# A graph kernel of four layers, last layer: the order in which its last five row blocks are prepared, summed and finished

## The chip, the cores and the metric

The kernel runs on one core of a Trainium2 chip. A core has five engines that run side by side, each through its own queue of instructions in order: TensorE (PE in the profile, with PEld for its weight loads), VectorE (DVE), ScalarE (ACT), GpSimd (POOL) and SyncE (SP), which here only starts DMA transfers. An instruction waits for semaphores that other engines or transfers raise, and what stands behind it on the same engine waits with it. The metric is the device time of one launch in microseconds; lower is better.

## The reference

Four layers work on a feature matrix `x` of 2708 rows and 512 columns with one sparse adjacency matrix `adj` of 2708 by 2708. Each layer is a sum over neighbours, a nonlinearity, and a residual with layer normalisation. Only the last layer matters here:

```python
bw = sign(weight)                     # 512 x 512
ba = maximum(sign(x), 0)
xw = ba @ bw.T                        # whole numbers
x  = layernorm(x + relu(adj @ xw))    # mean and variance of a row, eps 1e-5
```

## The kernel before

The rows are cut into 22 blocks of 128 (block 21 has 20). The adjacency matrix is never multiplied whole. For a block `b`, the columns that hold anything were listed in the first layer, and the matching rows of `adj` were packed into `packed[b]`, tiles of 128 listed columns by the block's rows. `ROOM[b]` is the number of such tiles, `DIRECT` names column tiles that are taken whole. In the last layer `xw_rows` in memory holds `xw` in 16 bit.

**Sums.** A block's sum `l3_b` is built on PE in one bank of PSUM (pool `ps_3`, three of them). It consists of:

- its own diagonal: `dp` (two matrices, a high and a low part of the diagonal, made by ACT at L2122 and by DVE at L2125) times its own rows `xo`, fetched by SP at L2114 and widened to 32 bit by `widened`, which uses DVE every third time (L2036) and ACT otherwise (L2038). The products are at L2130;
- its tiles: four at a time, `halves_of` splits `packed[b]` into a high half (ACT, L2025) and a low half (DVE, L2026), and each tile is multiplied twice (L2141) with the rows that POOL gathered (`gather3`, L626) or with rows that lie in SBUF.

The five densest blocks, 0 to 4, are not gathered. Their five sums (`whole`, five banks) grow together, one column tile at a time, in `whole_tile(j)`: 22 steps of ten products (L2102), spread between the other blocks by a count of tiles (`due`). The last of the 22 falls after block 15, so blocks 16 to 20 run with nothing between them.

**Finishing.** `finish3(b, ps, more)` adds the relu of the sum to the old features (L2049), takes the statistics of a row (L2051, L2053), and notes them in `moments`. With `more` it stops there, so that the next block joins it. Otherwise it takes the root for the one or two blocks noted: the constant is added (L2060), ACT takes a square root (L663), DVE improves its reciprocal in a few tiny steps (`newton`, L680 to L683) and forms the offset (L2062). ACT then scales each block (L2066) and SP writes it out (L2070). In the tail before the change the pairs are 15 and 16, 17 and 0, 18 and 1, 19 and 2, then 20 alone, then 3 and 4.

**Order.** The code above is traced in program order, and a scheduler then arranges the instructions of each engine by estimated times; it moves work of a later block ahead of an earlier one and the reverse. `in_order()` is a context in which each engine keeps the traced order: every instruction gets an ordering edge to the one traced before it on its engine. Before the change it is used in the first layer, not here. SP's transfers take part in this as well: a DMA issue is an instruction of SP's queue.

**Buffers** that the tail uses: `xo` 2, `dp` 2, widened rows 4, split halves (`parts`) 4, gathered tiles 11, sums 3, `rs3` 2, `mv3` 3.

Of the kernel before, what the change touches and what calls it, by code (L numbers as in the profile page):

```python
# [8 lines left out]
F32 = mybir.dt.float32  # L9
# [4 lines left out]
AF = mybir.ActivationFunctionType  # L14
ALU = mybir.AluOpType
# [4 lines left out]
P = 128  # L20
# [39 lines left out]
WHOLE3 = 5  # L60
# [447 lines left out]
def sparse_layers(ctx, tc, x, adj, adj_t, w0_t, b0, w_sa, a_sa, w_gcnb, b_gcnb, wa, ba, wb, bb, w3_t,  # L508
# [11 lines left out]
    nc = tc.nc  # L520
    N, D = x.shape
    KC = D // P
    NB = -(-N // P)
# [4 lines left out]
    def rows(b: int) -> int:  # L528
        return min(P, N - b * P)

    def direct(b: int):

        return tuple(range(NB)) if b == 0 else DIRECT.get(b, ())

    def tiles(b: int) -> int:
        return len(direct(b)) + ROOM[b]
# [3 lines left out]
    small = ctx.enter_context(tc.tile_pool(name="s_small", bufs=4))  # L540
    dram = ctx.enter_context(tc.tile_pool(name="s_dram", bufs=1, space=DRAM))

    f = [feat.tile([P, D], F32, tag=f"f{b}", name=f"f{b}") for b in range(NB)]
# [115 lines left out]
    def rsqrt_of(dst, v, m: int, n: int, name: str):  # L659

        r = small.tile([P, 2, 4], F32, tag="rsqs", name=f"rsqs_{name}")
        r0, r1 = r[:m, 0, :n], r[:m, 1, :n]
        nc.scalar.activation(r0, v, AF.Sqrt)  # L663
        newton(dst, v, r0, r1, n)

    def newton(dst, v, r0, r1, n: int):

        for step_ in newton_steps(dst, v, r0, r1, n):
            step_()
# [49 lines left out]
    with tc.tile_pool(name="s_pre", bufs=1) as pre:  # L719
# [33 lines left out]
        for d in (y_rows, x1_rows, x2_rows, xw_rows):  # L753
# [16 lines left out]
            out=tri, in_=tri, pattern=[[1, P]], compare_op=ALU.is_gt, fill=0.0, base=0,  # L770
# [5 lines left out]
            out=step, in_=ident, pattern=[[1, P]], compare_op=ALU.not_equal, fill=-1.0,  # L776
# [8 lines left out]
        turn_at, at = {}, 0  # L785
# [35 lines left out]
        b = 0  # L821
        while b < NB:
# [6 lines left out]
            b = end  # L829
# [1184 lines left out]
    with tc.tile_pool(name="s_l3", bufs=11, reuse_waits="tile") as lp, \  # L2014
            tc.tile_pool(name="s_ps_w", bufs=1, reuse_waits="tile", space=PSUM) as ps_w, \
            tc.tile_pool(name="s_ps_3", bufs=3, reuse_waits="tile", space=PSUM) as ps_3:
        W3 = WHOLE3 * P
        CH3 = 4
        PW = max(CH3 * P, W3)

        def halves_of(a, r: int, w: int, name: str):

            p = lp.tile([P, 2, PW], F32R, tag="parts", name=f"p{name}", bufs=4)
            low, high = p[:r, 0, :w], p[:r, 1, :w]
            nc.scalar.copy(high, a)  # L2025
            nc.vector.tensor_tensor(low, a, high.bitcast(F32), op=ALU.subtract)  # L2026
            return p

        turn = [0]

        def widened(t, r: int, name: str, tag: str = "wide", bufs: int = 4):

            g = lp.tile([P, D], F32R, tag=tag, name=f"w{name}", bufs=bufs)
            turn[0] += 1
            if turn[0] % 3 == 0:
                nc.vector.tensor_copy(g[:r], t[:r])  # L2036
            else:
                nc.scalar.copy(g[:r], t[:r])  # L2038
            return g

        moments = []

        def finish3(b: int, ps, more: bool):

            m = rows(b)
            old = place_of_x(b)
            k = len(moments)
            t = old[:, :D]
            nc.vector.scalar_tensor_tensor(t[:m], ps[:m], 0.0, t[:m], op0=ALU.max, op1=ALU.add)  # L2049
            st = small.tile([P, 6], F32, tag="st", name=f"st_3_{b}")  # L2050
            nc.vector.bn_stats(st[:m], t[:m])  # L2051
            mv = moments[0][2] if k else lp.tile([P, 2, 2], F32, tag="mv3", name=f"mv_3_{b}", bufs=3)
            nc.vector.bn_aggr(mv[:m, k, :], st[:m])  # L2053
            moments.append((b, t, mv))
            if more:
                return
            n = len(moments)
            rs = lp.tile([P, 2, 2], F32, tag="rs3", name=f"rs_3_{b}", bufs=2)
            mean, v = mv[:m, :n, 0], mv[:m, :n, 1]
            nc.vector.tensor_scalar(v, v, LN_EPS, None, op0=ALU.add)  # L2060
            rsqrt_of(rs[:m, 0, :n], v, m, n, f"3_{b}")
            nc.vector.scalar_tensor_tensor(  # L2062
                rs[:m, 1, :n], mean, -1.0, rs[:m, 0, :n], op0=ALU.mult, op1=ALU.mult
            )
            for k, (b, t, _) in enumerate(moments):
                nc.scalar.activation(  # L2066
                    t[:m], t[:m], AF.Identity, bias=rs[:m, 1, k : k + 1],
                    scale=rs[:m, 0, k : k + 1],
                )
                nc.sync.dma_start(out[b * P : b * P + m, :], t[:m])  # L2070
            moments.clear()

        sources3 = {}

        def gather3(b: int):
            sources3[b] = [gathered(lp, D, xw_rows, b, t, F32R) for t in range(ROOM[b])]

        order3 = [NB - 1, *range(WHOLE3, NB - 1)]
        gather3(order3[0])
        gather3(order3[1])  # L2080


        whole = [ps_w.tile([P, D], F32, tag=f"w{b}", name=f"l3_{b}") for b in range(WHOLE3)]

        xw_direct = {0: xw0}

        def whole_tile(j: int):
            r = rows(j)
            if j:
                g = lp.tile([P, D], F16, tag="xs", name=f"xs{j}", bufs=4)  # L2090
                nc.sync.dma_start(g[:r], xw_rows[j * P : j * P + r, :])
                g = widened(g, r, f"s{j}", "wide" if j > 1 else "wide1", 4 if j > 1 else 1)
                if j == 1:
                    xw_direct[1] = g
            else:
                g = xw0
            a = lp.tile([P, W3], F32, tag="aw", name=f"aw{j}", bufs=4)
            nc.sync.dma_start(a[:r], adj_t[j * P : j * P + r, :W3])
            p = halves_of(a[:r], r, W3, f"w{j}")
            for b in range(WHOLE3):  # L2100
                for h in range(2):
                    nc.tensor.matmul(  # L2102
                        whole[b], p[:r, h, b * P : (b + 1) * P], g[:r, :],
                        start=(j == 0 and h == 0), stop=(j == NB - 1 and h == 1),
                    )
        j = 0
        while j < AHEAD3:
            whole_tile(j)
            j += 1
        due = 0  # L2110
        for at, b in enumerate(order3):
            m = rows(b)
            xo = lp.tile([P, D], F16, tag="xo", name=f"xo{b}", bufs=2)
            nc.sync.dma_start(xo[:m], xw_rows[b * P : b * P + m, :])  # L2114
            xo = widened(xo, m, f"o{b}")
            if at + 1 < len(order3) and at:
                gather3(order3[at + 1])
            src = [xw_direct[j] for j in direct(b)] + sources3.pop(b)
            ps = ps_3.tile([P, D], F32, tag="mm", name=f"l3_{b}")

            dp = lp.tile([P, 2, P], F32R, tag="dp", name=f"dp{b}", bufs=2)
            nc.scalar.activation(  # L2122
                dp[:m, 1, :m], ident[:m, :m], AF.Copy, scale=dia_own[:m, b : b + 1]
            )
            nc.vector.scalar_tensor_tensor(  # L2125
                dp[:m, 0, :m], ident[:m, :m], dia_own[:m, b : b + 1],
                dp[:m, 1, :m].bitcast(F32), op0=ALU.mult, op1=ALU.subtract,
            )
            for h in range(2):
                nc.tensor.matmul(  # L2130
                    ps[:m], dp[:m, h, :m], xo[:m, :], start=(h == 0), stop=False
                )
            for i0 in range(0, tiles(b), CH3):
                n = min(CH3, tiles(b) - i0)
                p = halves_of(
                    packed[b][:, i0 : i0 + n, :].rearrange("p n i -> p (n i)"), P, n * m,
                    f"{b}_{i0}",
                )
                for i in range(n):
                    for h in range(2):  # L2140
                        nc.tensor.matmul(  # L2141
                            ps[:m], p[:, h, i * m : (i + 1) * m], src[i0 + i],
                            start=False, stop=(i0 + i == len(src) - 1 and h == 1),
                        )
            pending = bool(moments)
            finish3(b, ps, not pending and b not in (order3[0], order3[-1]))
            if j == NB and whole and len(moments) == 1:
                finish3(WHOLE3 - len(whole), whole.pop(0), False)
            due += ROOM[b]
            while j < NB and due >= FETCHES3:  # L2150
                whole_tile(j)
                j += 1
                due -= FETCHES3
        while whole:
            finish3(WHOLE3 - len(whole), whole.pop(0), len(whole) % 2 == 1)


@with_exitstack
# [74 lines left out]
```

## Time and profile before

| what | value |
|---|---|
| median of 9 runs | 957.8 us (954.47 to 960.23) |
| the profiled execution's own time | 955.83 us |
| its span | 954.0 us |
| mean granted TensorE clock | 0.961 |
| busy: PE, DVE, POOL, ACT | 852.7, 648.0, 548.1, 382.8 us |
| last layer's sums, first product to last | about 837.5 to 942.2 us |
| last block of the whole tiles ends | 924.4 us |
| last output issued | 948.5 us |

The span is the time from the first to the last event of the core; the execution's own time has 1.83 us more around it. Times in the profile count from the span's start. In lists of groups or of a timeline a line reads: start and length in us, engine, line of the program, operation, the tile written, an arrow, the tiles read, sizes, and the number of instructions merged into the line. In brackets stands how long the engine had been idle before it and what released it. `SPq` marks the issue of a transfer on SP's queue. Timeline lines of one kind that follow each other on their engine are merged, so a length can include short gaps. Matmul ends are modelled.

### The profile page before, as it was taken

How to read it: one execution, taken by the hardware profiler on the slowest of the kernel's cores; microseconds unless marked ns; L12 is line 12 of the kernel's file. 1: busy time of each engine (PE TensorE's matmuls, PEld its weight loads, DVE VectorE, ACT ScalarE, POOL GpSimd, SP SyncE). 2: the span in 40 equal slices, each digit the busy share in tenths (PEclk: the TensorE clock that was granted, in tenths of full speed). 3: DMA queues.
4: the chain of work that ended last, by engine and by line, in shares of the span. 5: the costliest groups of instructions: out<-in, count | busy, mean ns of one | idle time of the engine just before them, and what ended most of it. 6: DMA issues, size and time to landing. Idle time of an engine off the chain costs nothing.

```text
span 954.0 us, 12778 instructions
## 1 busy us (share of the span) xinstructions
PE 852.7 (89%) x3659; PEld 449.4 (47%) x3659; DVE 648.0 (68%) x2440; ACT 382.8 (40%) x812; POOL 548.1 (57%) x660
## 2 busy tenths in 40 slices
PE   1897998589999989999999979989999999689993
PEld 1444553122223334565555534544556455368872
DVE  4898887846677846556544447576888776557676
ACT  2675665100000115545444434334444433255664
POOL 2688888788888577777532054543454320067662
PEclk9999899889999979999999999999999999889998
DMA  9999996567777657776643277886787541299985
GB/s 264 363 344 328 351 309 189 165 199 219 229 226 231 207 167 209 219 239 207 191 151 122 101 259 262 277 283 230 238 304 258 171 145 49 83 299 353 342 250 191
DMA packets 93556, 220.05 MB, mean 231 GB/s; under 512 B 13660, under 2 KB 28364, under 8 KB 93476
## 3 DMA queue, kind: packets, MB, share of 16 engines
q0 software_dynamic: 43008, 127.61, 44.5%
q1 hardware_dynamic: 38520, 76.78, 23.5%
q10 hardware_dynamic: 11948, 14.76, 4.9%
q8 instruction: 31, 0.51, 0.2%
q14 instruction: 49, 0.40, 0.1%
HBM read 178.21 MB, written 31.71 MB: 220 GB/s over the span
## 4 chain that ended last, share of the span: by engine, by line
PE 65%; DMA 10%; DVE 9%; POOL 5%; issue 3%; ACT 1%; SPq 0%; ACTq 0%; DVEq 0%; POOLq 0%
PE l L1396 15%; PE h L1622 8%; PE e L1847 6%; PE a L1847 6%; PE l L2102 6%; PE l L2141 4%; PE pg L1895 4%; PE pc L1895 3%; DMA xg<-y_rows,i 3%; DMA arow<-in_adj_dram 2%; PE e L1655 2%; PE a L1656 2%; POOL a L1099 2%; DMA xg<-x_rows,i 2%; PE px L1956 2%
## 5 line engine op out<-in xcount | busy, mean ns | idle before, releaser
L1099 POOL DMA_INDIRECT a<-in_adj_t_dram,row_at x98 | 108.0, 1102 | 49.7 <-issue 21.7
L626 POOL DMA_INDIRECT xg<-x_rows,i x98 | 96.2, 982 | 66.7 <-PE l L1396 39.4
L626 POOL DMA_INDIRECT xg<-y_rows,i x98 | 98.7, 1007 | 25.3 <-issue 18.2
L1396 PE MATMUL l<-xg,a 128*32 128x512 f32 (+3 forms) x196 | 92.6, 624 | 16.7 <-DMA xg<-y_rows,i 16.5
L1823 POOL DMA_INDIRECT xg<-x_rows,i x60 | 59.5, 992 | 61.2 <-ACT ae L1578 16.5
L626 POOL DMA_INDIRECT xg<-xw_rows,i x70 | 70.9, 1012 | 35.4 <-issue 12.0
L1823 POOL DMA_INDIRECT a<-x_rows,i x38 | 37.1, 977 | 88.8 <-DVE mask L1581 37.0
L1133 PE MATMUL y<-s_w,xt 128*128 128x512 f32 (+1 forms) x176 | 87.1, 641 | 0.0
L1622 PE MATMUL h<-s_wsa,xt 128*128 128x256 f32 (+3 forms) x352 | 81.9, 385 | 0.0
L1622 PEld LDWEIGHTS h<-s_wsa,xt 128*128 128x128 f32 (+1 forms) x352 | 63.8, 186 | 24.8 <-ACT xt L1617 12.5
L840 ACT ACTIVATE unused<-arow 128x1408 uint8<-128x1408 f32 (+3 forms) x44 | 58.5, 1329 | 11.9 <-DMA arow<-in_adj_dram 6.7
L1847 PE MATMUL a<-xg,a 128*32 128x512 f32 (+2 forms) x120 | 48.9, 609 | 4.5 <-DMA xg<-x_rows,i 4.5
L663 ACT ACTIVATE rsqs<-mv 128x1 f32<-128x1 f32 (+2 forms) x56 | 11.3, 202 | 101.9 <-DVE mv L692 97.8
L1133 PEld LDWEIGHTS y<-s_w,xt 128*128 128x128 f32 (+1 forms) x176 | 33.8, 203 | 37.5 <-issue 37.2
L1396 PEld LDWEIGHTS l<-xg,a 128*32 128x32 f32 (+3 forms) x196 | 20.6, 143 | 64.9 <-DMA xg<-y_rows,i 44.8
L2102 PE MATMUL l<-ws,pw 128*128 128x512 f32 (+1 forms) x210 | 50.1, 392 | 0.0
L1847 PE MATMUL e<-xg,ae 128*32 128x512 f32 (+2 forms) x120 | 47.9, 601 | 1.3 <-ACT ae L1583 1.3
L694 POOL TENSOR_TENSOR rs<-mv,s_neg_half 128x1 f32<-128x1 f32 (+1 forms) x22 | 13.0, 590 | 60.0 <-DVE mv L692 51.1
L1895 PE MATMUL pg<-s_wg,pt 128*128 128x256 f32 (+1 forms) x176 | 44.8, 395 | 1.3 <-ACT pt L1883 1.3
L688 DVE BATCH_NORM_STATS2 st<-t 128x6 f32<-128x512 f32 (+1 forms) x66 | 45.3, 686 | 0.3
L904 DVE TENSOR_SCALAR s_mask<-arow 128x1300 bf16<-128x1300 f32 (+5 forms) x42 | 38.0, 910 | 9.8 <-DMA arow<-in_adj_dram 9.8
L2102 PEld LDWEIGHTS l<-ws,pw 128*128 128x128 f32 (+1 forms) x210 | 39.7, 190 | 8.8 <-DVE rs L2062 0.4
(310 smaller groups left out, 1958.4 us busy)
## 6 DMA issues: line engine op xcount, KB each, us to landing
arow<-in_adj_dram SPq DMA_DIRECT2D x21, 704.0 KB, 7.4
arow<-in_adj_dram SPq DMA_DIRECT2D x21, 650.0 KB, 6.5
x_rows<-f SPq DMA_DIRECT2D x40, 256.0 KB, 3.7
aw<-in_adj_t_dram SPq DMA_DIRECT2D x21, 320.0 KB, 4.2
y_rows<-yt ACTq DMA_DIRECT2D x20, 256.0 KB, 5.5
x_rows<-h SPq DMA_DIRECT2D x19, 257.0 KB, 2.6
f<-in_x_dram SPq DMA_DIRECT2D x19, 256.0 KB, 7.1
h_own<-x_rows SPq DMA_DIRECT2D x19, 256.0 KB
```

Source lines behind the costliest of these rows:

```text
L626: nc.gpsimd.indirect_dma_start(out=t, out_offset=None, in_=src[:, :], in_offset=bass.IndirectOffsetOnAxis(ap=index[b][:, i : i + 1], axis=0),)
L688: nc.vector.bn_stats(st[:m], t[:m])
L840: nc.scalar.activation(unused[:m, : ar.shape[1]], ar, AF.Copy, accum_out=row_sums[:m, b, h : h + 1])
L1099: nc.gpsimd.indirect_dma_start(out=packed[b][:, t + len(direct(b)), :], out_offset=None, in_=adj_t, in_offset=bass.IndirectOffsetOnAxis(ap ...
L1133: nc.tensor.matmul(ps[:m], xt[:, k, :m], w0[:, k, :], start=(k == 0), stop=(k == KC - 1))
L1396: nc.tensor.matmul(ps[r0:r1], weights, moving, start=(i == order[0]), stop=last_of(b, i, order))
L1622: nc.tensor.matmul(ps, xt[:, k, :m], w[:, k, :], start=(k == 0), stop=(k == KC - 1))
L1823: nc.gpsimd.indirect_dma_start(out=g, out_offset=None, in_=x2_rows[:, :], in_offset=bass.IndirectOffsetOnAxis(ap=index[b][:, t : t + 1], a ...
L1847: nc.tensor.matmul(ps[r0:r1], weights, moving, start=(i == order[0]), stop=last_of(b, i, order))
L1895: nc.tensor.matmul(ps, pt[:, k, :m], w[:, k, :], start=(k == 0), stop=(k == KC - 1))
L2102: nc.tensor.matmul(whole[b], p[:r, h, b * P : (b + 1) * P], g[:r, :], start=(j == 0 and h == 0), stop=(j == NB - 1 and h == 1),)
L2141: nc.tensor.matmul(ps[:m], p[:, h, i * m : (i + 1) * m], src[i0 + i], start=False, stop=(i0 + i == len(src) - 1 and h == 1),)
```

## The change

The body of the loop over the blocks is cut into functions, and the loop is split in two. Up to block 15 (while column tiles of the whole blocks are left) a block is done as before: `ready` (own rows and diagonal), the next block's gathers, `products3` (which splits the tiles four at a time as it goes), `finish3`.

For blocks 16 to 20 everything is traced inside `in_order()`:

- `all_parts(b)` makes all operands of a block: the fetch of its own rows, their widening, its diagonal, both halves of all its tiles. It is called for block 16 before the loop, and for block `b + 1` after the products of `b` and ahead of the finishing of `b`.
- `finish3` takes the square root on ACT, then calls `between`, and only then does the tiny steps, the scaling and the output. In blocks 16 to 19 `between` is the first half of finishing one whole block (sum, statistics), which stays in `moments` for the next turn.
- The pairs are now 15 and 16, 0 and 17, 1 and 18, 2 and 19, then 3 and 4, then 20 alone.

```diff
-        def finish3(b: int, ps, more: bool):
+        def finish3(b: int, ps, more: bool, between=None):
...
             n = len(moments)
+            done = list(moments)
+            moments.clear()
...
-            rsqrt_of(rs[:m, 0, :n], v, m, n, f"3_{b}")
-            nc.vector.scalar_tensor_tensor(
-                rs[:m, 1, :n], mean, -1.0, rs[:m, 0, :n], op0=ALU.mult, op1=ALU.mult
-            )
-            for k, (b, t, _) in enumerate(moments):
...
+            r = small.tile([P, 2, 4], F32, tag="rsqs", name=f"rsqs_3_{b}")
+            r0, r1 = r[:m, 0, :n], r[:m, 1, :n]
+            nc.scalar.activation(r0, v, AF.Sqrt)
+
+            def apply():
+                newton(rs[:m, 0, :n], v, r0, r1, n)
+                nc.vector.scalar_tensor_tensor(
+                    rs[:m, 1, :n], mean, -1.0, rs[:m, 0, :n], op0=ALU.mult, op1=ALU.mult
+                )
+                for k, (b, t, _) in enumerate(done):
+                    nc.scalar.activation(
+                        t[:m], t[:m], AF.Identity, bias=rs[:m, 1, k : k + 1],
+                        scale=rs[:m, 0, k : k + 1],
+                    )
+                    nc.sync.dma_start(out[b * P : b * P + m, :], t[:m])
+
+            if between:
+                between()
+            apply()
...
-        for at, b in enumerate(order3):
+        ready3 = {}
+
+        def ready(b: int):
             m = rows(b)
             xo = lp.tile([P, D], F16, tag="xo", name=f"xo{b}", bufs=2)
             nc.sync.dma_start(xo[:m], xw_rows[b * P : b * P + m, :])
             xo = widened(xo, m, f"o{b}")
...
+            ready3[b] = (xo, dp, [])
+
+        def ready_part(b: int, i0: int):
+            n = min(CH3, tiles(b) - i0)
+            ready3[b][2].append(halves_of(
+                packed[b][:, i0 : i0 + n, :].rearrange("p n i -> p (n i)"), P, n * rows(b),
+                f"{b}_{i0}",
+            ))
...
+        def all_parts(b: int):
+            ready(b)
             for i0 in range(0, tiles(b), CH3):
...
+                ready_part(b, i0)
...
+        at = 0
+        while j < NB:
+            b = order3[at]
+            ready(b)
+            if at:
+                gather3(order3[at + 1])
+            ps = products3(b)
+            finish3(b, ps, not moments and at > 0)
+            at += 1
             due += ROOM[b]
             while j < NB and due >= FETCHES3:
                 whole_tile(j)
                 j += 1
                 due -= FETCHES3
-        while whole:
-            finish3(WHOLE3 - len(whole), whole.pop(0), len(whole) % 2 == 1)
+
+        def finish_whole(more: bool):
+            finish3(WHOLE3 - len(whole), whole.pop(0), more)
+
+        with in_order():
+            all_parts(order3[at])
+            while at < len(order3):
+                b = order3[at]
+                at += 1
+                if at < len(order3):
+                    gather3(order3[at])
+                ps = products3(b)
+                if at < len(order3):
+                    all_parts(order3[at])
+                else:
+                    while whole:
+                        finish_whole(len(whole) > 1 and not moments)
+                left = whole and at < len(order3)
+                finish3(
+                    b, ps, not moments and at < len(order3),
+                    (lambda: finish_whole(True)) if left else None,
+                )
```

More of the change, by code (lines that the diff above doesn't have):

```diff
@@ L2060, in finish3 @@
             nc.vector.tensor_scalar(v, v, LN_EPS, None, op0=ALU.add)
-            rsqrt_of(rs[:m, 0, :n], v, m, n, f"3_{b}")
-            nc.vector.scalar_tensor_tensor(
-                rs[:m, 1, :n], mean, -1.0, rs[:m, 0, :n], op0=ALU.mult, op1=ALU.mult
-            )
-            for k, (b, t, _) in enumerate(moments):
-                nc.scalar.activation(
-                    t[:m], t[:m], AF.Identity, bias=rs[:m, 1, k : k + 1],
-                    scale=rs[:m, 0, k : k + 1],
-                )
-                nc.sync.dma_start(out[b * P : b * P + m, :], t[:m])
-            moments.clear()
+            r = small.tile([P, 2, 4], F32, tag="rsqs", name=f"rsqs_3_{b}")
[5 more added lines that the diff above has]
+                    rs[:m, 1, :n], mean, -1.0, rs[:m, 0, :n], op0=ALU.mult, op1=ALU.mult
+                )
+                for k, (b, t, _) in enumerate(done):
[7 more added lines that the diff above has]
+            apply()
         sources3 = {}
@@ L2115, in sparse_layers @@
             xo = widened(xo, m, f"o{b}")
[L2116 to L2119, printed above, removed]
             dp = lp.tile([P, 2, P], F32R, tag="dp", name=f"dp{b}", bufs=2)
@@ L2128, in sparse_layers, with products3 @@
             )
+            ready3[b] = (xo, dp, [])
[5 more added lines that the diff above has]
+            ))
+        def products3(b: int):
+            m = rows(b)
+            src = [xw_direct[j] for j in direct(b)] + sources3.pop(b)
+            ps = ps_3.tile([P, D], F32, tag="mm", name=f"l3_{b}")
+            xo, dp, parts = ready3.pop(b)
             for h in range(2):
@@ L2132, in sparse_layers @@
                 )
-            for i0 in range(0, tiles(b), CH3):
[L2134 to L2148, printed above, removed]
+            for i in range(tiles(b)):
+                if i // CH3 == len(parts):
+                    ready3[b] = (xo, dp, parts)
+                    ready_part(b, i)
+                    ready3.pop(b)
+                p, k = parts[i // CH3], i % CH3
+                for h in range(2):
+                    nc.tensor.matmul(
+                        ps[:m], p[:, h, k * m : (k + 1) * m], src[i],
+                        start=False, stop=(i == len(src) - 1 and h == 1),
+                    )
+            return ps
+        def all_parts(b: int):
+            ready(b)
+            for i0 in range(0, tiles(b), CH3):
+                ready_part(b, i0)
[8 more added lines that the diff above has]
+            at += 1
             due += ROOM[b]
```

## The prediction

> **What bounds the kernel now.** I read the slices of the page first, then the busy times over two stretches of the end, then the chain of waits, then the timeline of the same stretch engine by engine. The change touches only what is issued for blocks 16 to 20, so the end is what matters.
>
> Two stretches (start:end, length, then busy us and instruction count of PE, weight loads, DVE, ACT, POOL, then PE clock, DMA share, GB/s):
>
> ```profile
> 920.00:940.00 20.00, 16.73 (x65) 12.70 (x63) 17.81 (x63) 9.95 (x22) 10.65 (x11) 0.91 0.80 225
> 940.00:954.00 14.00, 2.13 (x8) 1.42 (x8) 5.92 (x31) 6.50 (x11) 0.00 (x0) 0.69 0.47 174
> ```
>
> PE is all but done at 940. DVE is the fuller engine in the last 20 us: 17.81 of 20. The chain of waits (start, us) says the same:
>
> ```profile
> 929.44 2.30 PE l L2141 x10
> 935.42 1.19 DVE st L2051 x2
> 940.07 2.14 PE l L2141 x8
> 942.96 1.29 DVE st L2051 x2
> ```
>
> So the end is already a DVE chain, with one excursion to PE: the last block's products. The timeline shows why PE stood still before it:
>
> ```profile
> 939.33 0.69 DVE L2026 TENSOR_TENSOR p<-a,p 128x512 fp32r<-128x512 f32 x1
> 940.07 0.73 PE L2141 MATMUL l<-xw,p 128*128 128x512 f32 x2 [3.35 <-DVE p L2026]
> ```
>
> The low half of block 20's operand stood on DVE behind the finishing of 16 to 19, and PE waited 3.35 us for it. That is the visible prize. Next, one pair being finished (13 and 14), which gives the prices of the steps, and the outputs on SP's queue that follow it:
>
> ```profile
> 918.43 0.68 DVE L2051 BATCH_NORM_STATS2 st<-f 128x6 f32<-128x512 f32 x1
> 919.14 0.18 DVE L2053 BATCH_NORM_AGGREGATE mv<-st 128x2 f32<-128x6 f32 x1
> 919.36 0.17 DVE L2060 TENSOR_SCALAR mv<-mv 128x2 f32<-128x2 f32 x1
> ...
> 919.72 0.20 ACT L663 ACTIVATE rsqs<-mv 128x2 f32<-128x2 f32 x1
> ...
> 920.01 0.15 DVE L680 RECIPROCAL rsqs<-rsqs 128x2 f32<-128x2 f32 x1
> ...
> 921.63 0.16 DVE L2062 SCALAR_TENSOR_TENSOR rs<-mv,rs 128x2 f32<-128x2 f32 x1
> 921.83 1.52 ACT L2066 ACTIVATE f<-f,rs 128x512 f32<-128x512 f32 x2
> ```
>
> ```profile
> 913.23 0.33 SPq L2114 DMA_DIRECT2D xo<-xw_rows  x1
> 915.40 0.33 SPq L2114 DMA_DIRECT2D xo<-xw_rows  x1
> 920.11 0.80 SPq L2114 DMA_DIRECT2D xo<-xw_rows  x2
> 922.67 1.04 SPq L2070 DMA_DIRECT2D out_dram<-f  x2
> ```
>
> What to see: the four loads of xo, for blocks 17 to 20, are all issued before the outputs of 13 and 14. No block of the tail waits for its own rows. DMA issues of the end (KB each, median us to landing):
>
> ```profile
> out_dram<-f SPq DMA_DIRECT2D x13, 256.0 KB, 3.0
> xs<-xw_rows SPq DMA_DIRECT2D x20, 128.0 KB, 4.4
> ```
>
> **The change part by part.** Laying the two built orders beside each other: on all five engines nothing moves up to block 15, apart from line numbers, and no instruction is added or dropped. The split of the root (square root, then the rest after the whole block) and the new pairs (15+16, 0+17, 1+18, 2+19, 3+4, 20 alone) keep six roots in the tail, as before. These edits cost nothing by themselves; everything lies in the order of 16 to 20.
>
> *The prize.* Block b+1's operands now stand ahead of block b's finishing, so the 3.35 us of PE disappear.
>
> *SP's queue.* The order is now: xo17, outputs 13, 14, 15, 16, xo18, outputs 0, 17, xo19, outputs 1, 18, xo20, and so on. SP issues in order, and an output waits for its L2066 on ACT. So xo18 is issued only when block 16 is finished, xo19 only after 17, xo20 only after 18. Behind xo18 stands a widening on DVE, at the head of DVE's order, and behind that dp18, p18 and all of block 17's finishing. For xo19 and xo20 the widening is on ACT, ahead of dp and p there, and DVE's dp, p and the next finishing wait for ACT. That is a closed loop: finish b-1, output, load xo of b+1, operands of b+1, finish b. Nothing runs ahead of it.
>
> *One turn of the loop*, from L2049 of block b to L2049 of b+1. L2049 to statistics 0.72 (942.24 to 942.96, block 20), to aggregate 0.71, to the added constant 0.22 (rows above): 1.65. Then the whole block in between: 0.10 to its L2049, 0.72, 0.71, and 0.20 to the reciprocal: 3.38. The root on ACT (0.36 + 0.29) hides under the whole block's 1.7 us. From the reciprocal to L2062 five steps of 0.20 (921.04, 921.23, 921.43, 921.63 are such starts), 1.0; 0.20 to ACT: 4.58. From ACT's first L2066 to the end of the second output's issue 1.88 (921.83 to 923.71), 0.10 to xo's issue: 6.56. Landing: the trace has no landing for xo. Bounds are 2.0 us, the fastest DMA that touches x_rows, and 4.4, the median of xs, the same rows and size at a DMA share over 1. I take 3.0, the outputs' own median here, because the queue is as empty in the loop as in this stretch: 9.56. Then the operands. With DVE widening: 0.46, dp 0.40, p 0.69, so 1.55. With ACT widening: 0.53, dp 0.33, high half 0.62, then DVE's low half 0.75, so 2.25 (starts at 914.23, 914.76, 915.28; lengths of L2025 and L2026). A turn is 11.1 us for 18, and 11.8 for 19 and 20.
>
> *The sum.* Block 16's products end where they did: whole tile 21 still ends at 924.4, the half clock from 924.8 to 928.1 remains, and p16 is ready at 924.0. L2049 of 16 stays at 929.0. Then 17 at 929.0 + 11.1 = 940.1, 18 at 951.9, 19 at 963.7. From there: 4.38 to L2062 of pair 2+19 (968.1). Block 4 follows: 0.1 + 0.72 + 0.71 + 0.22 + 0.36 + 0.29 + 1.0 = 3.4 (971.5). Block 20: 0.1 + 0.72 + 0.71 + 0.22 + 0.36 + 0.29 + 0.8 (one column, four steps) = 3.2 (974.7). Then 0.2 to ACT, 0.8 for L2066, 0.05 to the issue: 975.75. In the trace of before the last output is issued at 948.52 and the span ends at 954.0, 5.48 later: 981.2. That is 27.2 us over 954.0. The profiled execution took 955.83, 1.83 around its span, and the median of the nine is 957.8. I add the difference to the median: 985.0.
>
> *What is covered.* The whole blocks' five L2049, which ran from 922.09 while PE was busy, now stand inside the turns; they are counted there. Gathers (POOL) of 18 to 20 wait for tiles that 15 to 17 release, by 931.7, some 8 us before use. PE's products of a block are ten; at half clock they take 0.38 each (3.04 for 8 at 925.95) to 0.52, at most 5.2 us, and DVE comes to them a turn later. For block 20 they run from about 963 to 969 and are wanted at 971.6; if this cover went, each us past 971.6 would be a us.
>
> *Rule against row, clock.* PE now stands idle 6 to 8 us a turn. Here the granted clock fell to 0.50 from 945.4, 3.1 us after PE's last product, and did not fall in the idle 3.35 us before 940.07. The Trainium skill ("TensorE: Matmul & The Clock Gate", "What's actually happening") puts the loss at one idle window of about 3.4 us, which speaks against this change: every block's products from 18 on would run at half speed. By the rows, half clock adds up to 2.6 us to PE's part of a turn and nothing to the sum above.
>
> *Rule against row, DMA.* The Trainium skill ("DMA: Bandwidth & Descriptors", "Anatomy of one DMA — SWDGE (gpsimd) path") gives about 2.0 us plus bytes over 436 GB/s, so an estimate of 2.3 us for 128 KB. By it three loads would be 2.1 us less in all, 982.9.
>
> **The rivals.** *The loads don't hold the loop.* If xo18 to xo20 came early after all, the in-order chain of DVE and ACT remains: 4.58 + 1.52 for the two L2066 + 2.25 = 8.3 a turn with ACT widening, 5.95 with DVE's (DVE goes on as soon as L2062 is done: 4.4 + 1.55). L2049 of 19 would be at 929.0 + 5.95 + 8.3 + 8.3 = 951.5, the end at 969.0, so 973. For it: xo18's buffer comes free early, when the copy of 16 has run (914.76). Against: SP's order has the load behind the outputs.
>
> *The prize is all there is.* The end is shortened by the 3.35 us that PE no longer waits, 957.8 - 3.35 = 954.4. It decides if a turn costs DVE no more than its busy time of before and the outputs' waits don't reach xo, that is if a turn stays under PE's pace, 2.3 us a block (931.58, 933.85, 936.11 are starts of blocks). For it: the wait is real and its cause is removed. Against: the two blocks finished in a turn hold 4.4 us of dependent steps on DVE alone, and before, other chains filled these gaps.
>
> *Nothing changes*: the stall is removed and as much given back. It needs turns of about 3 us; no row gives that.
>
> **How the numbers follow.** Forecast 0.89, loads not holding 0.06, prize alone 0.03, nothing 0.02. Landing between 2.0 and 4.4 moves the forecast by -3.0 to +4.2; steps of 0.2 that are 0.17 or 0.25 move a turn by 0.3 to 0.5 and the tail by as much, some 2 us; the median itself wanders by 1 to 2. So 978 to 992 for the forecast, and this holds more than 8 in 10 without reaching to the others. About 0.2% is what a measurement of this kernel can tell from no change. Faster is the third case, 0.03, same 0.02, slower the rest, 0.95.
>
> **What would show it.** In the profile of after: SP issues of xo for 18, 19 and 20 some 11 to 12 us apart, each right after a pair of outputs; DVE idle before the widening of 18 with the DMA as releaser, ACT before those of 19 and 20; PE idle 6 us or more before the products of 18, 19 and 20, with the clock at 0.5 in the last two; L2049 of the last five blocks at about 929, 940, 952, 964, 972. I am wrong if the xo issues come close together near 920, if PE's products from 17 to 20 follow one another within 3 us, or if block 16 itself starts late, which would mean that something before the tail had moved.

## The result, and the profile after

| | before | changed |
|---|---|---|
| median | 957.34 us (31 runs, 951.93 to 961.34) | 981.61 us (10 runs, 977.18 to 984.1) |
| ratio, 95% interval | 1 | 1.0249 (1.0228 to 1.0270) |
| span of the profiled execution | 954.0 us | 980.0 us |
| mean granted clock | 0.961 | 0.946 |
| start of whole tile 21 (the 20-row weights) | 921.84 us | 924.26 us |
| from there to the end of the span | 32.16 us | 55.74 us |

The change makes the kernel slower by 24 us. Whole tile 21 is the last work that both kernels do in the same place. Up to it the two executions differ by 2.4 us, behind it by 23.6 us: the loss lies in the tail. (The 2.4 us arise ahead of the last layer, where the two kernels do the same: its first product comes at 837.53 before and at 840.83 after.)

The chain of waits of the changed kernel (start, us, then what the chain ran through; its last two lines of products and what follows them):

```profile
924.33 2.51 PE l L2112 x10
927.51 2.32 PE l L2162 x10
936.55 3.73 DMA xo<-xw_rows
947.88 2.40 DMA xo<-xw_rows
958.79 2.18 DMA xo<-xw_rows
```

Before, this chain ended in PE and DVE steps. Now it goes through three loads of xo, some 11 us apart. Why they start so late is seen in the issues on SP's queue, from the timeline (a merged line covers the gaps between its issues):

```profile
915.65 0.33 SPq L2127 DMA_DIRECT2D xo<-xw_rows  x1
924.96 11.24 SPq L2077 DMA_DIRECT2D out_dram<-f  x4
936.55 0.33 SPq L2127 DMA_DIRECT2D xo<-xw_rows  x1
946.79 0.33 SPq L2077 DMA_DIRECT2D out_dram<-f_other  x1
947.50 0.33 SPq L2077 DMA_DIRECT2D out_dram<-f  x1
947.88 0.45 SPq L2127 DMA_DIRECT2D xo<-xw_rows  x1
```

In before the last four loads stood ahead of the outputs of 13 and 14. Here each of the last three stands right behind a pair of outputs and goes out 0.05 to 0.35 us after the end of the second one's issue. The timeline of one turn on DVE and ACT, from block 17 to block 18 (in brackets the idle time before a line and what ended it):

```profile
941.51 0.68 DVE L2049 SCALAR_TENSOR_TENSOR f<-l,f 128x512 f32<-128x512 f32 x1
...
945.95 0.81 ACT L2073 ACTIVATE f_other<-f_other,rs 128x512 f32<-128x512 f32 x1 [2.37 <-DVE rs L2069]
...
950.30 0.62 ACT L2038 CAST wo<-xo 128x512 fp32r<-128x512 f16 x1 [2.83 <-DMA xo<-xw_rows]
...
951.66 1.22 PE L2152 MATMUL l<-wo,dp 128*128 128x512 f32 x2 [5.98 <-DVE dp L2133]
...
952.37 0.69 DVE L2049 SCALAR_TENSOR_TENSOR f<-l,f 128x512 f32<-128x512 f32 x1
```

The turn closes on itself: sum of 17, scaling 4.44 us later, output, load of block 19's rows (issued 6.37 us after the sum), widening 2.42 us after the issue, and 2.07 us after that the sum of 18, which stands behind 19's operands in DVE's order. PE had been idle 5.98 us before 19's first products. The busy times by stretch (start:end, length, then busy us of PE, weight loads, DVE, ACT, POOL, then clock, DMA share, GB/s) show that none of the five engines is full:

```profile
936.00:940.00 4.00, 0.00 (x0) 0.00 (x0) 0.00 (x0) 0.65 (x2) 0.94 (x1) 0.53 1.06 313
940.00:944.00 4.00, 2.95 (x7) 2.38 (x8) 3.56 (x9) 0.20 (x1) 0.00 (x0) 0.50 0.01 1
944.00:948.00 4.00, 1.68 (x4) 0.77 (x3) 1.71 (x8) 1.52 (x2) 0.00 (x0) 0.50 0.09 35
948.00:952.00 4.00, 0.34 (x1) 0.34 (x2) 0.59 (x2) 1.43 (x3) 0.00 (x0) 0.50 0.38 129
```

DVE, which had 17.81 us of work in the 20 us before 940 in the kernel before, is busy 5.86 of these 16 us. The DMA engines are full in the first stretch only (a share of 1.06), with gathers of the last blocks and outputs. The rest of the tail is bound by latency: by steps that wait for one another.

One of the profiles used below, that of `e1`, was taken in a slow execution (1014.03 us; the fastest of `e1` took 997.95), so its steps are read together with those of `e8`, which come from a fast one.

### The profile page after: what moved, and what is told of

It is laid out like the page before. It is cut to its first block, busy times and chain, and to the rows that moved or that the text cites. A ratio compares the mean times of both kernels' runs of the same rounds, so it can differ in the third digit from the quotient of the medians.

```text
span 980.0 us, 12773 instructions
## 1 busy us (share of the span) xinstructions
PE 860.2 (88%) x3659; PEld 452.5 (46%) x3659; DVE 655.1 (67%) x2440; ACT 382.6 (39%) x812; POOL 548.2 (56%) x660
## 4 chain that ended last, share of the span: by engine, by line
PE 62%; DMA 8%; DVE 8%; issue 2%; ACT 2%; POOL 2%; SPq 0%; ACTq 0%; DVEq 0%; POOLq 0%
PE l L1396 14%; PE h L1622 8%; PE a L1847 6%; PE e L1847 6%; PE l L2112 5%; PE pg L1895 4%; DMA xg<-y_rows,i 3%; PE pc L1895 3%; PE l L2162 3%; DMA xg<-x_rows,i 2%; PE e L1655 2%; PE a L1656 2%; PE px L1956 2%; PE l L1457 1%; PE xt1p L1615 1%
## 5 line engine op out<-in xcount | busy, mean ns | idle before, releaser
L1847 PE MATMUL a<-xg,a 128*32 128x512 f32 (+2 forms) x120 | 51.0, 628 | 4.0 <-DMA xg<-x_rows,i 4.0
L663 ACT ACTIVATE rsqs<-mv 128x1 f32<-128x1 f32 (+1 forms) x44 | 8.9, 203 | 99.0 <-DVE mv L692 98.4
```

The source lines that it names most:

```text
L1847: nc.tensor.matmul(ps[r0:r1], weights, moving, start=(i == order[0]), stop=last_of(b, i, order))
```

## The experiments

Chips differ: the kernel before took 995.6 us on the one that ran the four versions `e1`, `e3`, `e4` and `e5`, 957.6 on that of `e6` to `e9`, 985.8 on that of `e10` to `e12` and 985.5 on that of `e13`. So each time is given as a ratio to the kernel before on the same chip, and places in the traces as "tail", the time from the start of whole tile 21 to the end of the span (32.16 us before, 55.74 changed). A tail comes from a single execution, and some of them hold a stretch at half clock worth 1 to 1.6 us, which the last section describes. Line numbers shift by a few with each edit.

**The changed kernel again**, beside `e6` to `e8`.

> The changed kernel itself, beside the others on this chip: ratio 1.0249 as before.

1.0254 (1.0218 to 1.0290), tail 55.6 us. The loss repeats on another chip.

**Undo the whole idea: leave the split, take the traced order away** (`e3`).

```diff
-        with in_order():
+        if True:
```

> The changed kernel without the fixed order: the scheduler arranges the last five blocks; operands traced ahead, split root, whole blocks between, and the new pairs stay. In the built order all four loads of xo stand before the outputs of 13 and 14 again. Theory (the fixed order closes the loop; the rest costs nothing): 957.3 less up to 3.4 us for block 20's operand, which now stands earlier on DVE: 954 to 958. Rival (the new pairs and the operands ahead cost by themselves): 965 or more.

0.9981 (0.9945 to 1.0018), tail 31.8 us. All the new functions, the split root and the new pairs are still there; so they cost nothing that can be measured, and the 24 us belong to the order. What is left of the prize is also seen: PE waits less for block 20's operand.

```profile
978.42 0.73 PE L2152 MATMUL l<-wo,dp 128*128 128x512 f32 x2 [1.31 <-DVE dp L2133]
```

The wait was 3.35 us and is 1.31, but the tail is only 0.4 us shorter, and the ratio can't be told from 1. So by the tail the stall in the profile of before was not a loss of its own, as DVE worked through it; the interval of the ratio alone would still leave room for it.

**The order alone, on the code of before** (`e5`): `in_order()` entered once the last whole tile is done, operands made in their old place.

> The kernel before, with the last five blocks and the remaining whole blocks kept in their traced order, nothing else: operands of a block are traced after the finishing of the one before it. Theory (fixed order plus one queue for loads and outputs makes the loop, operands ahead shorten it): the products at half clock, 4 us, and the operands now stand in each turn too; turns of about 14 to 16 us from 17 on, 1000 to 1010. Rival (operands ahead and the new pairs make the loop, order alone does little): 957 to 965.

1.0497 (1.0449 to 1.0546), tail 80.2 us. Here too the loads stand behind the outputs, and in addition each block's operands stand behind the finishing of the one before. The first sums of 17 and 18, on DVE, and the products of 18 on PE:

```profile
969.72 0.69 DVE L2049 SCALAR_TENSOR_TENSOR f<-l,f 128x512 f32<-128x512 f32 x1 [3.73 <-PE l L2146]
...
984.11 0.69 DVE L2049 SCALAR_TENSOR_TENSOR f<-l,f 128x512 f32<-128x512 f32 x1 [4.13 <-PE l L2146]
```

```profile
979.44 1.22 PE L2135 MATMUL l<-wo,dp 128*128 128x512 f32 x2 [9.75 <-DVE dp L2130]
```

The turns are 14.0 to 15.1 us. So within a traced order the rest of the change (operands ahead, split root, new pairs, which are not told apart here) saves about half of what the order costs (1.0497 against 1.0249). It doesn't pay for it.

**Take the loads off SP's queue** (`e1`).

```diff
-            nc.sync.dma_start(xo[:m], xw_rows[b * P : b * P + m, :])
+            queue = nc.gpsimd if j == NB else nc.sync
+            queue.dma_start(xo[:m], xw_rows[b * P : b * P + m, :])
```

> The changed kernel, but the own rows (xo) of blocks 16 to 20 are fetched through POOL's queue instead of SP's, so no output stands ahead of them. Theory (outputs hold the loads, the loads hold the loop): the turn to 18 falls from 11.7 us to about 5.6 (4.3 to L2069, 0.1, then 1.2 for copy, dp and p on DVE), the turns to 19 and 20 from 10.9 and 10.7 to about 8.0 (4.4 to ACT's scaling, 1.5 for it, 2.1 from the widening to L2049); 11.6 us less, median about 970, ratio to before 1.013. Rival (the fixed order of DVE and ACT alone is the loss, the load only shows as the last wait): less than 3 us, 979 or more. Rival (the loads are the whole loss): back to 957.

1.0121 (1.0067 to 1.0175), tail 46.7 us. Half of the loss is gone with one line, and no instruction of the tail waits for the rows of xo any more (one wait of PE, 4.82 us before 18's products at 978.64, is put down to a gather, but their diagonal too was finished only at 978.59). What the turn is now bound by is one engine further, on ACT, and DVE shows it (timeline of ACT, then of DVE):

```profile
983.79 0.81 ACT L2073 ACTIVATE f_other<-f_other,rs 128x512 f32<-128x512 f32 x1 [2.37 <-DVE rs L2069]
984.51 0.80 ACT L2073 ACTIVATE f<-f,rs 128x512 f32<-128x512 f32 x1
985.22 0.60 ACT L2038 CAST wo<-xo 128x512 fp32r<-128x512 f16 x1
985.73 0.40 ACT L2131 ACTIVATE dp<-s_ident,s_dia_own 128x128 fp32r<-128x128 f32 x1
```

```profile
986.16 0.35 DVE L2134 SCALAR_TENSOR_TENSOR dp<-s_ident,s_dia_own,dp 128x128 fp32r<-128x128 f32 x1 [2.40 <-ACT dp L2131]
987.27 0.68 DVE L2049 SCALAR_TENSOR_TENSOR f<-l,f 128x512 f32<-128x512 f32 x1
```

The operands of the next block stand behind both scalings on ACT's own order, although the load of its rows (xo) had been issued 8.8 us before the widening, and nothing is seen to wait for it. The turns were 7.40, 7.92 and 7.93 us. The first, with the widening on DVE, was expected at 5.6 and missed: DVE's widening can go early, but the diagonal's first half (L2131) is on ACT, behind the scalings, in every turn. DVE's part of the diagonal waited 1.54 us for it there.

**Make the operands two blocks ahead** (`e8`, with the loads as in `e1`): `all_parts` is called for 16 and 17 first, then for `b + 2` behind the products of `b`.

> Fixed order, own rows through POOL's queue, and the operands of a block traced two blocks ahead instead of one, so that they no longer stand behind the preceding block's scaling on ACT. Theory (what is left without the held loads is ACT's scaling ahead of the operands, then DVE's own steps in a row): turns fall from 7.4, 7.9, 7.9 us to about 5.5 each; from the end of the whole tiles to the end of the span 5.6 + 16.5 + 16.9 = 39 us, 7 more than before: ratio 1.007. Rival (DVE's steps alone make the 7.9): no change to one ahead, 1.012.

1.0127 (1.0097 to 1.0157), tail 45.0 us. By the ratio no gain: the rival's value. The sums of 16 to 19:

```profile
931.57 0.68 DVE L2049 SCALAR_TENSOR_TENSOR f<-l,f 128x512 f32<-128x512 f32 x1
...
939.49 0.68 DVE L2049 SCALAR_TENSOR_TENSOR f<-l,f 128x512 f32<-128x512 f32 x1
...
947.40 0.68 DVE L2049 SCALAR_TENSOR_TENSOR f<-l,f 128x512 f32<-128x512 f32 x1
...
951.72 0.68 DVE L2049 SCALAR_TENSOR_TENSOR f<-l,f 128x512 f32<-128x512 f32 x1
```

The turns are 7.92, 7.91 and 4.32 us: the pace is that of `e1` as long as operands are made. The third turn is short because with two blocks ahead none are left to be made in it. Some 1.5 us of that are lost again to a stretch at half clock behind whole tile 21, which `e1` had not. In a full turn the trace has the same rows as `e1`:

```profile
944.64 0.80 ACT L2073 ACTIVATE f<-f,rs 128x512 f32<-128x512 f32 x1
945.35 0.60 ACT L2038 CAST wo<-xo 128x512 fp32r<-128x512 f16 x1
```

```profile
946.28 0.35 DVE L2134 SCALAR_TENSOR_TENSOR dp<-s_ident,s_dia_own,dp 128x128 fp32r<-128x128 f32 x1 [2.40 <-ACT dp L2131]
```

The labels moved by one block, the order on each engine did not: on ACT the operands still follow the scaling of the block before, and on DVE they still precede the next sum. A distance of two blocks breaks nothing in a turn while two engines visit the same pair of steps in the same alternation.

**Move the operands to the other side of the scaling** (`e10`, as `e8`, but `all_parts(b + 2)` stands in `between`, behind the whole block's sum and ahead of the scaling).

```diff
...
+                def meanwhile(c=at + 1):
+                    finish_whole(True)
+                    if c < len(order3):
+                        all_parts(order3[c])
...
```

> The traced order kept, the loads of xo for blocks 16 to 20 through POOL's queue, and the operands made two blocks ahead, traced behind the whole block and ahead of the scaling, so that on ACT the identity scaling and the widening no longer stand behind the two scalings of the block before. Theory: with the loads on their own queue what is left of the turn is that loop over ACT (7.9 us a turn); with it broken only the DVE steps in a row are left, some 5.5 to 5.9 us a turn, and the time is about 7 us over the kernel before, ratio 1.0075. Rival: the turn is set by DVE's order alone, whichever place the operands have, so that the turn stays 7.9 and the ratio 1.0125.

1.0042 (1.0007 to 1.0076), tail 38.5 us. The turns were 5.52, 5.18 and 5.19 us, at the lower end of the 5.5 to 5.9 expected or a little under it; the rival's 7.9 and 1.0125 are out. On ACT the operands now come first, and DVE doesn't wait for the diagonal:

```profile
963.63 0.60 ACT L2038 CAST wo<-xo 128x512 fp32r<-128x512 f16 x1
964.14 0.40 ACT L2131 ACTIVATE dp<-s_ident,s_dia_own 128x128 fp32r<-128x128 f32 x1
966.95 0.82 ACT L2073 ACTIVATE f_other<-f_other,rs 128x512 f32<-128x512 f32 x1 [1.91 <-DVE rs L2069]
```

```profile
964.94 0.32 DVE L2134 SCALAR_TENSOR_TENSOR dp<-s_ident,s_dia_own,dp 128x128 fp32r<-128x128 f32 x1
```

Together these runs divide the loss. From the changed kernel (1.0249) to `e1` (1.0121), the loads behind outputs: 1.3%, some 12 us. From `e1` to `e10` (1.0042), the operands behind the scalings on ACT: 0.8%, some 8 us. From `e10` to `e3` (0.9981), what else the order holds in a row: 0.6%, some 6 us. In the three turns of `e10` DVE is busy 14.85 of 15.89 us, so what is left there is mostly DVE's own steps; the kernel before did four of the five whole blocks' sums (L2049, from 922.69 to 927.32) ahead of block 16's. How the 6 us divide further was not tested. By the tails of the profiled executions the three are 9.1, 8.2 and 6.7 us; the last would be some 1.5 us more if `e3` had been without the stretch at half clock, as the other three were. The intervals of single ratios are 0.3 to 0.5% to each side, so the shares are rough; that all three are there, and their order of size, is borne out by the turns and the tails.

**Take the whole block out of the chain** (`e4`): the tiny steps, scaling and outputs ahead of the whole block instead of behind it.

```diff
+            apply()
             if between:
                 between()
-            apply()
```

> The changed kernel, with the whole block's sum and statistics after the scaling instead of between root and scaling. Theory (what counts in a turn is only the way to the output's issue, since DVE then idles for the load): scaling starts 3.5 us after L2049 instead of 4.4, so 0.9 less in each of three turns, 0.6 more in the last: about 2 us less, 979.5. Rival (DVE's work bounds the turn, filling its gap with the whole block helps): slower than 981.6 by 2 us or more, since the root's 0.65 us is no longer hidden in each turn.

1.0193 (1.0142 to 1.0243), tail 51.6 us. The direction was right, the size was too small: 4.1 us of tail instead of 2. The scaling starts 3.29 us after the sum instead of 4.44, in every turn, and the whole block then lies under the load's flight, where DVE had nothing else to do. The turns were 9.41, 9.67 and 9.52, together 4.6 us less than in the changed kernel. Of these 3.5 are the earlier scaling; 1.1 came from the first load, which was used 2.68 us after its issue instead of 3.75, and 0.5 are lost again at the end.

**Keep PE busy in the idle time** (`e6`): 30 products of `xw0` by itself into the sum's tile, written over by the products that count, ahead of the products of 18, 19 and 20.

> The changed kernel with 30 unused products (xw0 by itself, 0.23 us each at full clock, overwritten by the block's own) ahead of the products of blocks 18, 19 and 20, so that PE doesn't stand idle long enough to lose its clock. Theory (PE at half clock is off the path, DVE comes to its products a turn later): no change to the changed kernel within 2 us. Rival (half clock is part of the loss): the three blocks' 3.6 us fall to 2.0 and the time falls by 3 to 5 us.

1.0258 (1.0216 to 1.0299): no change. The clock did what it was to do, and nothing came of it. The same stretch as above, of `e6`, and its first sums of 18 and 19, which the changed kernel has at 952.37 and 963.06:

```profile
948.00:952.00 4.00, 2.96 (x13) 1.85 (x11) 0.92 (x2) 1.43 (x3) 0.00 (x0) 1.00 0.31 100
```

```profile
952.04 0.68 DVE L2049 SCALAR_TENSOR_TENSOR f<-l,f 128x512 f32<-128x512 f32 x1
...
962.87 0.68 DVE L2049 SCALAR_TENSOR_TENSOR f<-l,f 128x512 f32<-128x512 f32 x1
```

Full clock against half moved the sums by 0.2 to 0.3 us, about what they were ahead at block 16 already (929.62 against 929.85).

**Look for a version that beats both.** The other four start from `e3`, since DVE is full there to the end.

`e7`: the whole blocks' relu on ACT and their sum on POOL.

```diff
...
+            if b < WHOLE3:
+                r = lp.tile([P, D], F32, tag="rl", name=f"rl_{b}", bufs=2)
+                nc.scalar.activation(r, ps, AF.Relu)
+                nc.gpsimd.tensor_tensor(t, r, t, op=ALU.add)
...
```

> Without the fixed order, and the whole blocks' relu is taken by ACT and their sum by POOL instead of both by DVE (5 x 0.69 us off DVE). Theory (without the fixed order the tail is bound by DVE's work, PE's 3.35 us of waiting were no loss of their own): 2 to 3 us faster than the kernel without the fixed order, ratio to before 0.994 to 0.997. Rival (the tail is bound by PE's products and the last block's steps): no change to it, 0.998.

1.0044 (1.0023 to 1.0065), tail 37.2 us against 31.8 for `e3`: slower, a miss. The work left DVE and DVE got slower (POOL, then DVE):

```profile
924.60 2.53 POOL L2052 TENSOR_TENSOR f_other<-rl,f_other 128x512 f32<-128x512 f32 x2
...
932.22 1.32 POOL L2052 TENSOR_TENSOR f<-rl,f 128x512 f32<-128x512 f32 x1
```

```profile
924.72 2.57 DVE L2026 TENSOR_TENSOR p<-a,p 128x128 fp32r<-128x128 f32 x1 [0.27 <-ACT p L2025]
...
931.58 1.99 DVE L2069 TENSOR_SCALAR mv<-mv 128x2 f32<-128x2 f32 x1
```

The first DVE line takes 0.29 us elsewhere in this trace, the second 0.17. Each ends within 0.2 us of the POOL instruction beside it; with a third such place (3.11 us for a step of 0.16) DVE loses some 7 us (2.3 + 1.8 + 2.9), against 3.4 saved.

`e11`: the five whole blocks' sums left out.

> The changed kernel without its traced order, and with the sum of relu and residual (L2049) of the five whole blocks 0 to 4 left out, so these blocks' outputs are those of another computation. Theory: in the tail DVE is the bound, which is why the 2 us of PE's waiting that this version saves did not show; five sums of 0.68 us less are then 3.4 us less: ratio 0.9945. Rival: the tail is bound by the last block's chain over PE, and DVE has slack: the ratio stays 0.998.

0.9999 (0.9968 to 1.0031), tail 29.9 us. The theory's 0.9945 lies outside the interval, so DVE is not the bound alone. The tail is 1.9 us shorter than that of `e3`, but `e3` had a stretch at half clock behind whole tile 21, which `e11` had not and which is worth nearly as much. Whether any of the 3.4 us is gained can't be settled with runs that scatter by 1% on this chip.

`e12`: four buffers for `rs3`, and the scalings of blocks 3 and 19 on DVE.

> The changed kernel without its traced order, with four buffers instead of two for the scale and shift of the last layer (DVE waited 1.12 us for one of them at the last block), and with the scalings of blocks 3 and 19 on DVE instead of ACT (five of them stood in a row on ACT at the end, 3.63 us). Theory: the very end is a row on ACT that DVE can share once the sums are done: 1.5 to 2 us less than without these two edits, ratio 0.996. Rival: DVE is the bound to the end, and what is moved onto it takes back what ACT saves: 0.998.

0.9968 (0.9929 to 1.0006), tail 30.4 us, against 31.8 for `e3`. The five scalings in a row on ACT became three there and two on DVE, and DVE no longer waits for a buffer. But here too `e3` had the stretch at half clock, which `e12` had not, worth about as much. The interval holds 1 and the theory's 0.996 alike: not settled.

`e13`: as `e12`, in groups of four, four and three blocks, with the scalings of 4 and 20 on DVE.

> The changed kernel without its traced order, with four buffers for scale and shift, the last rows finished in groups of four, four and three (15+16+0+17, 1+18+2+19, 3+4+20) instead of five pairs and one alone, so with three roots instead of six, and the last two scalings (4 and 20) on DVE. Theory: DVE is nearly full in the tail and the roots are small steps on it, 1.1 us of busy time each: three fewer are 3.4 us of DVE, of which some 1 to 2 us show in the end, as with the five sums left out; about 29 us from whole tile 21 to the end instead of the 30.4 with the pairs, 0.995 of the time before. Rival: the last rows now wait for each other, three outputs go out at the very end instead of one, and that takes the gain back: 30.4 us or more, 0.997 to 1.0.

0.9988 (0.9962 to 1.0014), tail 35.0 us. The rival's value: three roots fewer on DVE bring nothing that can be measured. The tail is longer than those of `e3`, `e11` and `e12`; but from 944 to 952 its clock was 0.70 and 0.87, so this one trace doesn't tell how much the groups cost. No version was measured faster than the kernel before. A version that keeps the loads on SP's queue and traces them ahead of the outputs was not tried.

## Why the prediction was right

*The closed loop through SP's queue.* Shown. The queue's order was as read from the two built orders, the loads of 18, 19 and 20 were issued 11.3 and 10.9 us apart, right behind pairs of outputs, and taking them off this queue (`e1`) gave back half of the loss. It is the place in the queue that counts and not the queue: in `e3` the loads are on SP's queue too, ahead of the outputs, and nothing in its tail waits for them. The size was right as well: the prediction's two sums, 985 with the loads in the loop and 973 without, put 12 us on them, and `e1` measures 1.3%, some 12 us.

*One turn.* Its terms, against what the trace of the changed kernel has for the turns to 17, 18 and 19 (the first goes from block 16's sum):

| | predicted | measured |
|---|---|---|
| sum to the load's issue | 6.56 | 6.70, 6.37, 6.42 |
| landing, from issue to widening | 3.0 | 3.75, 2.42, 2.20 |
| operands to the next sum | 1.55, 2.25, 2.25 | 1.21, 2.07, 2.07 |
| the turn | 11.1, 11.8, 11.8 | 11.66, 10.86, 10.69 |

(The prediction's "turn for 18" is the turn that waits for the load of 18 and closes with the sum of 17, and so on; its places, 17 at 940.1, 18 at 951.9 and 19 at 963.7, are of the sums.) Two terms were mis-sized, each by 0.6 to 0.7 us over the three turns: the operands (5.35 us instead of 6.05) and the landing (8.37 instead of 9.0). The landing was long for the first load and short for the others. The prediction took the queue to be as empty in the loop as in the tail of before; the first load flew beside a DMA share of 1.06, the others beside 0.38 and 0.36 (means of 4 us). The Trainium skill ("DMA: Bandwidth & Descriptors", "Anatomy of one DMA — SWDGE (gpsimd) path"), from which the prediction took an estimate of 2.3 us, comes closer for the second and third and misses the first by 1.45 us; its rule is for transfers issued from GpSimd, and these were issued from SP.

*The sum.* 980.0 instead of 981.2, from four differences: whole tile 21 started 2.4 us later than in before, block 16's sum followed it after 5.59 us instead of 7.16, because the stretch at half clock that the prediction had carried over from before was absent, the turns were 1.5 us shorter, and the end behind block 19's sum took 16.94 instead of 17.5. That the first of these offset most of the others is luck; without it the span would have been 977.6. The median lies 3.4 us under the predicted 985.0: these 1.2, and 2.0 that were added because the profiled execution of before was faster than its median, while that of the changed kernel (981.83) was at its median.

*What is covered.* One reading was off, without effect on the sum: 922.09 in the trace of before is block 15's own sum; of the whole blocks' five, four ran from 922.69 on while PE was busy, and the fifth only at 940.08.

*The clock.* The half clock came: the granted clock fell to 0.50 between 936.0 and 936.5, 3.4 to 3.9 us after PE's last product, stayed there until about 956.6, and was at 0.50 again from about 960.3 to 967. So the products of 18, 19 and 20 all ran at half clock. It cost nothing that could be measured, as `e6` shows. The page that spoke against the change ("TensorE: Matmul & The Clock Gate", "What's actually happening", of the Trainium skill), which puts the loss at one idle window of about 3.4 us, was right about the clock here and without effect on the time.

*The prize.* Right that it would be swallowed. But it was priced as 3.35 us, and `e3`, which removes 2.0 us of that wait without the order, has a tail only 0.4 us shorter; its ratio, 0.9981, can neither show nor exclude a gain of 2 us.

*The rivals.* "The loads don't hold the loop" was priced at 973, with turns of 5.95 and 8.3. `e1` makes that case: 7.40 and 7.9. The 8.3 was near; the 5.95 failed at the step "DVE goes on as soon as L2062 is done": the diagonal's half on ACT holds that turn as well. By ratio `e1` stands for 969. "The prize is all" and "nothing changes" did not happen; their condition, turns near PE's pace of 2.3 us, is not met even by `e10`, whose turns are 5.2 to 5.5 us with loads and scalings out of the way.

## What to carry to other kernels

When an order is fixed by hand, write down for every in-order stream, DMA issue queues too, what stands ahead of the first instruction of the next block: a load that is traced behind an output waits for that output's whole chain, and a load's flight, 2 to 4 us here, then falls into every turn. Where the operands of the next block and the finish of the last one share two engines, look at their order on each engine, not at how many blocks ahead they are made: moving them two blocks ahead left the turn at 7.9 us, moving them ahead of the scaling brought it to 5.2. Don't price a wait of the matmul engine at its length when the engine that it waits for is full to the end: here 2.0 us less of waiting shortened the tail by 0.4.

## What was unexpected in the hardware

In `e7` POOL's float32 addition of two 128x512 tiles took 1.26 to 1.32 us, and DVE instructions beside it ended only with it: 128x2 steps of 0.16 and 0.17 us took 3.11 (beside two additions) and 1.99. The Trainium skill ("SBUF — State Buffer", "SBUF: two separate sides") says that a DVE operation with two SBUF inputs, or in a two-port mode, and a GpSimd operation take a shared pair of ports as an exclusive lock, each for its whole instruction, and that the one that starts first gets it. The ends agree with a lock, and show that steps of two elements per lane can be held as long as a 128x128 one. The starts agree in one place of three: the two 128x2 steps began, as recorded, 0.64 and 0.60 us before the addition (931.58 against 932.22, 936.56 against 937.16). Spans on POOL are rough, and this stays open.

A stretch of some 3 us at half clock behind whole tile 21 was in the traces of before, `e3`, `e5` and `e7` and, a little later, of `e8` and `e13`. It was not in those of the changed kernel, its repeat `e9`, `e1`, `e4`, `e6`, `e10`, `e11` and `e12`. The same window in before and in the changed kernel:

```profile
924.00:928.00 4.00, 4.00 (x11) 2.92 (x10) 3.12 (x7) 1.73 (x4) 1.43 (x2) 0.59 0.78 235
924.00:928.00 4.00, 4.00 (x17) 2.79 (x16) 3.01 (x8) 3.24 (x7) 2.51 (x3) 1.00 0.89 256
```

PE was full in both, so idleness there doesn't explain it. Its cause was not looked for. By block 16's eight products (3.04 us in before, 2.00 in the changed kernel) and the distance from tile 21 to its sum (7.16 and 5.59) it is worth 1 to 1.6 us of a tail, and it must be taken out before two traces are compared at that size.
